# Three edits in the seams of a fused decoder kernel: when the second up pass's weights are loaded, where the first down product stands, and idle transposes at the start

## The chip, the cores and the metric

The kernel runs on one core of one Trainium2 chip. The metric is the device time of one execution in microseconds. Times of before are the median of three runs; a profile is one further execution, taken with the hardware profiler.

## The reference

The layer takes `x` (16 x 112 rows of 1024) and `ctx` (16 x 375 rows of 1024), all fp32, and does three steps, each followed by a residual sum and a layer norm:

```python
# 1. gated MLP with a sparse gate (I = 2752)
s = silu(x @ w_gate.T)                       # 1792 x 2752
_, idx = top_k(-abs(s), 1376)                # the smaller half of each row ...
s = s.at[rows, idx].set(0.0)                 # ... is set to zero
y = (s * (x @ w_up.T)) @ w_down.T            # called h below: s * up
x = layernorm(x + y)
# 2. cross attention: 32 heads of 32, 8 key and value heads, softmax over 375 keys
x = layernorm(x + attention(x, ctx) @ Wo)
# 3. an int4 weight, unpacked with scales and zeros, in bf16
x = layernorm(x + x.astype(bf16) @ dequantized.T)
```

## The kernel before

The 1792 rows are 14 tiles of 128 (`TT = 14`). Everything runs on one core, and the order of the instructions on each engine is the order in which the program writes them (`as_written` ties each instruction to the one before it on its engine). Nothing is reordered later, so an instruction that waits holds up all that stands behind it on its engine. That holds for SP too, whose queue issues most DMAs.

**Stages.** First the gate: for each tile six chunks of columns, each 8 logical matmuls over the contraction, 16 on the engine, since an fp32 matmul is run as two (line 190). The chunk's sigmoid is taken on ScalarE (L199), multiplied on VectorE (L200) and stored to `s_d` in DRAM by GpSimd's queue (L201). Then the up product, by a Strassen scheme on pairs of tiles: four passes over the columns (`UPASS = 4`), seven pairs of tiles in each, so 28 units; each unit is seven products (`up_unit`, L297) of four logical matmuls. Then keys and values (`kv_unit`, L367 and L375), amid which h is formed: GpSimd multiplies s by its mask (`next_turn`, L421), TensorE transposes the chunk (`turn`, L439), ScalarE copies it out of PSUM (L441, L445) and SP stores it to `hT_d` (L213). Then the down product (class `Down`, L725), again by Strassen, then the layer norm, the query projection, attention, and the quantized layer.

**The search beside it.** From the second tile on, ScalarE and VectorE search each row's median of |s| bit by bit (`count`, L468 and L471; `update`, L479 and L480), and `beside` interleaves this search with the TensorE stream. A product's evacuation from PSUM stands in the program one stream step behind the product (`settle(1)`), among the search's own instructions. There are six PSUM banks for products (`ps_g`) and two for transposes (`ps_t`).

**The swap.** When the gate's weights are no longer needed, `swap` gives their space to the up stage and issues on SP, in this order: `load_rest(0)` (tile xl of unit 0, L252 and L253), `load_weights(1)` (the four weight blocks of pass 1, L229). The first step of unit 0 then issues four loads of s (`load_s`, tile us, L276) and, in `side_loads(0)`, `load_first(1)` (tile xe of unit 1, L245 and L246) and `load_rest(1)`. Weights of pass p are combined by GpSimd in `sum_weights(p)` (L239); for pass 1 that is at unit 2, and pass 1 begins at unit 7. Pass 0's weights were loaded earlier, during the gate. Later passes' weights are asked for at the second unit of the pass before.

**The turn to the down product.** At the end of `gates_up_keys` a loop runs `next_turn` until every chunk of h has been asked for, with the stores that fall due (`issue(0)`). Then `down.first_blocks()` issues the loads of the first three blocks of h (L711, L712). A second loop finishes the turns that are still open, and a last `issue(0)` their stores. Then `first_passes` runs the 14 products of the first two Strassen terms, in the order of `self.order`, with three blocks ahead; at each step SP issues one more block and three loads of the other half's weights (`b12`, `b22`, L768). These weights lie in space that the up stage's tiles had. At the step `s == 9` VectorE combines them (L732, L741). Each product is 11 logical matmuls, 22 on the engine.

**The start.** `load_x(0)` (L162) issues the first tile of x, then nine DMAs issue the gate's weights, the first chunk in four pieces (L586); the matmuls begin when the first piece has landed. `ident`, the identity for transposes, is made by GpSimd ahead of that.

Of the kernel before, what the change touches and what calls it, by code (L numbers as in the profile page):

```python
# [10 lines left out]
F32 = mybir.dt.float32  # L11
# [11 lines left out]
P = 128  # L23
# [24 lines left out]
UPASS = 4  # L48
# [58 lines left out]
def gates_up_keys(  # L107
# [37 lines left out]
    def room(pool, tag, name, size, *shape, bufs=1):  # L145

        a = pool.tile([P, size], F32, tag=tag, name=name, bufs=bufs)
        n = 1
        for d in shape:
            n *= d  # L150
        a = a[:, :n]
        if len(shape) == 2:
            return a.rearrange("p (a b) -> p a b", b=shape[1])
        if len(shape) == 3:
            return a.rearrange("p (a b c) -> p a b c", b=shape[1], c=shape[2])
        return a
# [3 lines left out]
    def load_x(t):  # L160
        xts[t] = room(io, "e", f"xT_{t}", 4 * KH * P, KC, P, bufs=2)
        nc.sync.dma_start(xts[t], xT[t])  # L162
# [48 lines left out]
    def issue(behind=2):  # L211
        while stores and stores[0][0] >= len(stream) + behind:
            nc.sync.dma_start(*stores.popleft()[1:])  # L213
# [6 lines left out]
    def load_weights(p):  # L220

        if p % 2:
            u = room(upool[0], "w0", f"u0_{p}", 3 * KH * UW, 3, KH, UW)
            v = room(upool[0], "w1", f"u1_{p}", 4 * KH * UW, 4, KH, UW)
        else:
            u = room(lo, "lo0", f"u0_{p}", 5120, 3, KH, UW)
            v = room(lo, "lo1", f"u1_{p}", 5632, 4, KH, UW)
        for to, k, h in ((u[:, 0], 0, 0), (u[:, 2], 0, 1), (v[:, 0], 1, 0), (v[:, 1], 1, 1)):
            nc.sync.dma_start(to, wu[:, ts(k, KH), ds(h * FH + p * UW, UW)])  # L229
        w_up[p] = u, v  # L230

    def sum_weights(p):
        u, v = w_up[p]
        b11, t1, b12, b21, b22, t2, t4 = (
            z.rearrange("p k n -> p (k n)")
            for z in (u[:, 0], u[:, 1], u[:, 2], v[:, 0], v[:, 1], v[:, 2], v[:, 3])
        )
        for to, x, y in ((t1, b12, b11), (t2, b22, t1), (b12, b22, b12), (t4, b21, t2)):
            nc.gpsimd.tensor_tensor(to, x, y, ALU.subtract)  # L239

    def load_first(i):

        j = i % pairs
        a = first[i] = room(io, "e", f"xe_{i}", 4 * KH * P, 4, KH * P, bufs=2)
        nc.sync.dma_start(a[:, :2], xT[2 * j].rearrange("p (h k) n -> p h (k n)", h=2))  # L245
        nc.sync.dma_start(a[:, 2:], xs_d[j].rearrange("p h k n -> p h (k n)")[:, :2])  # L246

    def load_rest(i):

        j = i % pairs  # L250
        a = rest[i] = room(upool[0], "l", f"xl_{i}", 3 * KH * P, 3, KH * P, bufs=2)
        nc.sync.dma_start(a[:, :2], xs_d[j].rearrange("p h k n -> p h (k n)")[:, 2:])  # L252
        nc.sync.dma_start(a[:, 2], xT[2 * j + 1][:, KH:].rearrange("p k n -> p (k n)"))  # L253

    def side_loads(i):
        if i + 1 < n_up:
            load_first(i + 1)
            load_rest(i + 1)
        p, at = divmod(i, pairs)
        if at == 1 and 0 < p < UPASS - 1:  # L260
            load_weights(p + 1)
        if at == (4 if p else 2) and p < UPASS - 1:
            sum_weights(p + 1)
        if i == n_up - 4:
            load_keys()
# [13 lines left out]
    def up_unit(i, what):  # L279
# [10 lines left out]
        if what == "A11 B11":  # L290
            if i == 0:
                for _ in range(4):
                    load_s()
            side_loads(i)
# [49 lines left out]
    def load_keys():  # L344
        kv["k"] = upool[0].tile([P, KC, KVD], F32, tag="wk", name="wk_sb")
        nc.sync.dma_start(kv["k"], wk)
        load_ctx(0)
# [67 lines left out]
    def next_turn():  # L415

        if ready:
            turn(*ready.popleft())
        if asked:
            t, c, s, m = asked.popleft()  # L420
            nc.gpsimd.tensor_tensor(s, s, m, ALU.mult)  # L421
            ready.append((t, c, s))
        load_turn()
        if len(asked) < 2:
            load_turn()
# [122 lines left out]
    def swap():  # L548
        w_ctx.close()
        upool.append(w_ctx.enter_context(tc.tile_pool(name="u_w", bufs=1, side="right")))  # L550
        load_rest(0)
        load_weights(1)

    stream = deque()
    for t in range(TT):
        for c in range(len(GATE_CHUNKS)):
            stream.append((GATE_CHUNKS[c][1], lambda t=t, c=c: gate_chunk(t, c)))
    stream.append((0, swap))
    for i in range(n_up):
        for what in ("A11 B11", "S2 T2", "A12 B21", "S1 T1", "S4 B22", "S3 T3", "A22 T4"):  # L560
# [20 lines left out]
        return w  # L581

    load_x(0)
    for off, w in GATE_CHUNKS:
        for k in ([ts(i, 2) for i in range(KC // 2)] if off == 0 else [slice(0, KC)]):
            nc.sync.dma_start(wg_sb[:, k, ds(off, w)], wg[:, k, ds(off, w)])  # L586
# [53 lines left out]
    while to_turn:  # L640
        next_turn()
        issue(0)
    down.first_blocks()
    while asked or ready:
        next_turn()
    issue(0)
# [3 lines left out]
class Down:  # L650
# [99 lines left out]
    def bank(self, name):  # L750
        return self.ps.tile([P, 512], F32, tag="pg", name=name)

    def first_passes(self):
        nc, tc = self.nc, self.tc
        acc = self.left.enter_context(tc.tile_pool(name="d_acc", bufs=1, side="left"))
        with ExitStack() as ctx:
            self.a2 = ctx.enter_context(tc.tile_pool(name="d_a2", bufs=1, side="left"))
            w = ctx.enter_context(tc.tile_pool(name="d_w", bufs=1, side="right"))
            n = self.pairs
            b12, b22, t2 = (w.tile([P, HK, 512], F32, tag=k, name=k) for k in ("b12", "b22", "t2"))  # L760
            self.c11, self.u, self.v = (
                [acc.tile([P, 512], F32, tag=f"{k}{j}", name=f"{k}_{j}") for j in range(n)]
                for k in ("c11", "u", "v")
            )

            def load_chunk(to, i, k):
                r = P if k < FULL else REST
                nc.sync.dma_start(to[:r, k, :], self.wd[ds(i * FH + k * P, r), 512:])  # L768

            others = deque((to, i, k) for k in range(HK) for i, to in enumerate((b12, b22)))  # L770
            for s, (j, h) in enumerate(self.order):
                if s + 3 < len(self.order):
                    jj, hh = self.order[s + 3]
                    self.ahead.append(self.block(2 * jj, hh))
                for _ in range(min(3, len(others))):
                    load_chunk(*others.popleft())
                if s == 9:
                    self.combine(nc.vector, b12, b22, b12, ALU.subtract)
                    self.combine_parts(
                        "11", lambda k, t: t2[:, k : k + t.shape[1]],  # L780
                        lambda k, t: b12[:, k : k + t.shape[1]], lambda k, t: t, ALU.add,
                    )
                if s == len(self.order) - 3:
                    self.load_sums(0)
                a = self.ahead.popleft()
                p = self.bank(f"m{1 + h}_{j}")
                self.product(p, a, lambda k: self.chunk(("11", "21")[h], k))
                if h == 0:
                    nc.scalar.copy(self.u[j], p)
                else:  # L790
                    nc.vector.tensor_add(self.c11[j], self.u[j], p)
            self.combine_parts(
                "11", lambda k, t: t, lambda k, t: b22[:, k : k + t.shape[1]],
                lambda k, t: t2[:, k : k + t.shape[1]], ALU.subtract,
            )
            self.combine_parts(
                "21", lambda k, t: t, lambda k, t: t2[:, k : k + t.shape[1]],
                lambda k, t: t, ALU.subtract,
            )
            for j in range(n):  # L800
                if j + 1 < n:
                    self.load_sums(j + 1)
                else:
                    self.a2 = None
                    self.load_rest(0)
                s2, s3, s4 = self.live.pop(j)
                p, q, r = (self.bank(f"m{i}_{j}") for i in (6, 3, 7))
                self.product(p, s2, lambda k: t2[:, k, :])
                nc.vector.tensor_add(self.u[j], self.u[j], p)
                self.product(q, s4, lambda k: b22[:, k, :])  # L810
                nc.vector.tensor_add(self.v[j], self.u[j], q)
                self.product(r, s3, lambda k: b12[:, k, :])
                nc.vector.tensor_add(self.u[j], self.u[j], r)
# [659 lines left out]
```

## Time and profile before

| | |
|---|---|
| median of 3 runs | 2603.91 us (2603.18 to 2606.75) |
| the profiled execution | 2605.19 us |
| its span, first to last instruction | 2603.4 us |
| mean granted TensorE clock | 0.987 |
| PE (matmul) busy | 97% of the span |
| VectorE, ScalarE, GpSimd busy | 66%, 53%, 46% |
| DMA | 478.65 MB, mean 184 GB/s |

The stages lie in the span as follows: gate from 6 to 526 us, up from 526 to 991, keys and values from 991 to 1361, down from 1375 to about 1846, attention and the quantized layer from there on. In the rows of the profile PE is a matmul or a transpose, PEld a weight load, DVE is VectorE, ACT ScalarE, POOL GpSimd, and SPq an issue on SP's queue. A timeline row gives start, length, engine, line, operation, tiles, and in brackets the idle time of the engine before it and what ended it. A stretch row gives the stretch, its length, the busy time and number of instructions of PE, PEld, DVE, ACT and POOL, the granted TensorE clock, the share of the DMA engines and GB/s. Busy times of PE are modelled in part; starts are more exact than ends.

### The profile page before, as it was taken

Reading aid. Unit: us, or ns where it says so; the run is one execution under the profiler, and the core shown is the slowest. Engines: PE = TensorE matmul, PEld = TensorE weight load, DVE = VectorE, ACT = ScalarE, POOL = GpSimd, SP = SyncE. Lnnn points to the kernel's source line nnn. Section 1 sums busy time; section 2 is a strip of 40 time slices with the busy share of each in tenths; the row PEclk is TensorE's granted clock in tenths of the full one; section 3 lists DMA queues with packets and bytes.
Section 4 is the critical chain, followed back from the end, with each engine's and each line's share of the span. In section 5 each row is a group of like instructions: output and inputs, shape, how many; then the busy total and the mean of one; then the engine's idle time right before and its main releaser. Section 6 shows DMA issues by size and latency. Waiting matters only on the chain.

```text
span 2603.4 us, 34755 instructions
## 1 busy us (share of the span) xinstructions
PE 2520.8 (97%) x10490; PEld 1524.5 (59%) x10490; DVE 1721.1 (66%) x3634; ACT 1390.9 (53%) x2470; POOL 1205.0 (46%) x1143
## 2 busy tenths in 40 slices
PE   9999999999999999999989999999889999999996
PEld 4444444456666666777764444444556666666763
DVE  0378778868888897677740343247577777777773
ACT  0487787767767877888830000000355555555652
POOL 1113333256457544454250000024387888878883
PEclk9999999999999999999998999999999999999998
DMA  6322322277768768988657223157587777777763
GB/s 243 134 70 87 109 105 84 88 254 239 233 228 278 232 232 274 302 282 290 224 173 254 87 85 111 54 189 231 148 209 186 204 187 198 192 194 197 193 178 95
DMA packets 283609, 478.65 MB, mean 184 GB/s; under 512 B 37856, under 2 KB 208224, under 8 KB 279328
## 3 DMA queue, kind: packets, MB, share of 16 engines
q1 hardware_dynamic: 241184, 374.06, 46.9%
q0 software_dynamic: 27008, 75.76, 9.4%
q10 hardware_dynamic: 15232, 26.62, 3.4%
q8 instruction: 85, 1.39, 0.2%
q14 instruction: 100, 0.82, 0.1%
HBM read 272.12 MB, written 103.50 MB: 144 GB/s over the span
## 4 chain that ended last, share of the span: by engine, by line
PE 49%; DMA 7%; DVE 6%; POOL 3%; ACT 3%; issue 3%; SPq 1%; ACTq 0%; POOLq 0%; DVEq 0%
PE m L725 14%; PE pu L297 7%; PE bank L1105 6%; PE bank L946 5%; PE pk L375 4%; PE pk L367 4%; PE sc L1013 3%; PE po L1068 3%; DMA weights<-squares 2%; PE bank L1156 2%; ACT probs L1021 1%; DMA hT_d<-hT 1%; DMA hm<-m_d 1%; DVE jv L471 1%; SPq L1055 1%
## 5 line engine op out<-in xcount | busy, mean ns | idle before, releaser
L468 ACT ACTIVATE ja<-a,cand 128x1824 int8<-128x1824 f32 x434 | 787.9, 1815 | 197.1 <-DVE cand L480 189.2
L471 DVE TENSOR_SCALAR_CACHE_REDUCE jv<-a,cand 128x928 uint8<-128x928 f32 x434 | 509.7, 1174 | 43.7 <-ACT a L455 36.7
L190 PE MATMUL pg<-wg_sb,xT 128*128 128x456 f32 (+1 forms) x1344 | 520.0, 550 | 6.0 <-DMA wg_sb<-in_wg_dram 6.0
L190 PEld LDWEIGHTS pg<-wg_sb,xT 128*128 128x128 f32 x1344 | 256.6, 191 | 268.7 <-issue 265.6
L1021 ACT ACTIVATE probs<-sc,nmax 128x375 f32<-128x375 f32 x512 | 286.3, 572 | 229.6 <-DVE nmax L1019 213.2
L1030 POOL TENSOR_TENSOR probs<-probs,sums 128x1500 f32<-128x1500 f32 x128 | 344.1, 2689 | 134.5 <-DVE sums L1029 91.5
L1019 DVE TENSOR_REDUCE nmax<-sc 128x2 f32<-128x750 f32 x256 | 228.5, 932 | 129.4 <-PE sc L1013 129.4
L297 PE MATMUL pu<-u,xe 128*128 128x344 f32 x896 | 265.9, 455 | 6.6 <-DMA xe<-in_xT_dram 4.3
L725 PE MATMUL m<-wd,h 128*128 128x512 f32 (+1 forms) x616 | 267.7, 597 | 2.6 <-DMA h<-hT_d 2.6
L1041 DVE STREAM_TRANSPOSE squares<-probs 128x1536 f32<-128x1536 f32 x128 | 224.0, 1750 | 20.8 <-DMA weights<-squares 10.3
L297 PEld LDWEIGHTS pu<-u,xe 128*128 128x128 f32 x896 | 170.9, 191 | 97.7 <-DVE cand L480 5.0
L201 POOL DMA_DIRECT2D s_d<-s x84 | 45.9, 546 | 361.5 <-DVE s L200 296.5
L946 PE MATMUL bank<-x1T,wq_sb 128*128 128x224 f32 x1008 | 210.1, 362 | 0.0
L946 PEld LDWEIGHTS bank<-x1T,wq_sb 128*128 128x128 f32 x1008 | 188.0, 192 | 34.2 <-issue 31.3
L725 PEld LDWEIGHTS m<-wd,h 128*128 128x128 f32 (+1 forms) x616 | 117.8, 192 | 151.2 <-issue 150.2
L297 PE MATMUL pu<-u,xl 128*128 128x344 f32 x672 | 199.6, 453 | 1.8 <-DVE c L330 1.4
L1105 PE MATMUL bank<-wo_sb,aT 128*128 128x256 f32 x832 | 194.6, 388 | 0.0
L939 ACT COPY x1T<-pq 128x448 f32<-128x448 f32 x4 | 1.9, 535 | 349.1 <-DMA sc<-in_qs_dram 330.9
L1105 PEld LDWEIGHTS bank<-wo_sb,aT 128*128 128x128 f32 x832 | 155.2, 191 | 45.8 <-issue 23.3
L1055 POOL DMA_DIRECT2D weights<-squares x320 | 177.9, 562 | 6.9 <-PE po L1068 2.4
L375 PE MATMUL pk<-wv_sb,ctx 128*128 128x256 f32 (+1 forms) x768 | 173.3, 379 | 0.0
L421 POOL TENSOR_TENSOR hs<-hs,hm 128x512 f32<-128x512 f32 (+1 forms) x84 | 97.8, 1173 | 161.8 <-DMA hm<-m_d 143.8
(150 smaller groups left out, 3369.0 us busy)
## 6 DMA issues: line engine op xcount, KB each, us to landing
weights<-squares SPq DMA_DIRECT2D x704, 96.0 KB, 3.5
h<-hT_d SPq DMA_DIRECT2D x56, 640.0 KB, 4.6
weights<-squares POOLq DMA_DIRECT2D x320, 96.0 KB, 3.6
ctx<-in_ctxT_dram SPq DMA_DIRECT2D x16, 1500.0 KB, 8.3
a<-s_d SPq DMA_DIRECT2D x14, 1376.0 KB, 8.3
us<-s_d SPq DMA_DIRECT2D x112, 172.0 KB, 3.9
u_d<-c SPq DMA_DIRECT2D x84, 172.0 KB, 3.5
xe<-in_xT_dram SPq DMA_DIRECT2D x28, 512.0 KB, 5.3
```

The source lines that it names most:

```text
L190: nc.tensor.matmul(pg[:, :w], xts[t][:, kc, :], wg_sb[:, kc, ds(off, w)], start=(kc == 0), stop=(kc == KC - 1),)
L297: nc.tensor.matmul(m, a[i][:, b, ts(n, P)], k[:, n, :], start=(n == 0), stop=(n == KH - 1))
L375: nc.tensor.matmul(pk[:n, :KVD], c[:, kc, ds(at, n)], kv["v"][:, kc, :], start=(kc == 0), stop=(kc == KC - 1),)
L468: nc.scalar.activation(ja, a[:, NV:], AF.Sign, bias=cand, scale=-1.0, accum_out=st["sgn"])
L471: nc.vector.tensor_scalar(jv, a[:, :NV], cand, -(TOPK - 1 - NA / 2), ALU.is_lt, ALU.add, accum_out=st["nlt"])
L725: self.nc.tensor.matmul(bank, a[:r, k, :], b(k)[:r], start=(k == 0), stop=(k == HK - 1),)
L946: nc.tensor.matmul(pq[:, :GT], self.wq_sb[:, kc, ts(mc, P)], self.x1T[g][:, kc, :], start=(kc == 0), stop=(kc == KC - 1),)
L1019: nc.vector.tensor_reduce(nmax[h], sc[h][:, :, :SK], AX.X, ALU.max, negate=True)
L1021: nc.scalar.activation(pr[:, i, :SK], sc[i // 2][:, i % 2, :SK], AF.Exp, bias=nmax[i // 2][:, i % 2 : i % 2 + 1], accum_out=sums[:, i : i ...
L1030: nc.gpsimd.tensor_tensor(pr, pr, sums.unsqueeze(2).to_broadcast([P, 4, SK]), ALU.mult)
L1041: nc.vector.transpose(sq[:, :, n % 2].rearrange("p k (i f) -> p k i f", f=Q), probs[:, n % 3].rearrange("p i (k f) -> p k i f", f=Q),)
L1105: nc.tensor.matmul(pp[:, :256], aT[:, h, r, :], wo_sb[:, h * REP + r, ts(i, 256)], start=(h == 0 and r == 0), stop=(h == 1 and r == REP - 1),)
```

## The change

Three edits:

1. `load_weights(1)` is no longer called in `swap`. It is called in `side_loads(0)`, so behind the us loads and behind `load_first(1)` and `load_rest(1)` on SP.
2. The first of the 14 products of `first_passes` is moved into a method `first_product`, which is called behind `first_blocks()` and ahead of the loop that finishes the last turns. Its evacuation stays in `first_passes`.
3. Behind `load_x(0)`, 24 transposes of `ident` into a PSUM tile that nobody reads are written, ahead of all other work of TensorE.

```diff
@@ side_loads
-        if at == 1 and 0 < p < UPASS - 1:
+        if at == (1 if p else 0) and p < UPASS - 1:
             load_weights(p + 1)
@@ swap
         load_rest(0)
-        load_weights(1)
@@ gates_up_keys
     load_x(0)
+
+    idle = ps_t.tile([P, 512], F32, tag="pt", name="idle")
+    for _ in range(24):
+        nc.tensor.transpose(idle[:, :P], ident, ident)
     for off, w in GATE_CHUNKS:
...
     down.first_blocks()
+    down.first_product()
     while asked or ready:
         next_turn()
     issue(0)
@@ Down
+    def first_product(self):
+
+        self.first = self.bank("m1_0")
+        self.product(self.first, self.ahead.popleft(), lambda k: self.chunk("11", k))
...
-                a = self.ahead.popleft()
-                p = self.bank(f"m{1 + h}_{j}")
-                self.product(p, a, lambda k: self.chunk(("11", "21")[h], k))
+                if s == 0:
+                    p = self.first
+                else:
+                    a = self.ahead.popleft()
+                    p = self.bank(f"m{1 + h}_{j}")
+                    self.product(p, a, lambda k: self.chunk(("11", "21")[h], k))
                 if h == 0:
                     nc.scalar.copy(self.u[j], p)
```

## The prediction

> **What bounds the kernel now.** I read the page first, then the waits of TensorE, then the three places that the diff touches in the timeline, with granted clock and DMA by stretch.
>
> ```profile
> PE 2520.8 (97%) x10490; PEld 1524.5 (59%) x10490; DVE 1721.1 (66%) x3634; ACT 1390.9 (53%) x2470; POOL 1205.0 (46%) x1143
> ```
>
> PE works 97% of 2603.4 us, so an edit pays only where PE stands still or runs slowly. Its few idle stretches include all three places.
>
> The swap from gates to up (timeline of PE and SP, then stretches with PEclk):
>
> ```profile
> 535.10 7.11 PE L297 MATMUL pu<-u,xl 128*128 128x344 f32 x24
> 546.53 11.18 PE L297 MATMUL pu<-u,xe 128*128 128x344 f32 x32 [4.33 <-DMA xe<-in_xT_dram]
> ...
> 526.41 1.03 SPq L253 DMA_DIRECT2D xl<-in_xT_dram  x1
> 527.48 2.89 SPq L229 DMA_DIRECT2D u<-in_wu_dram  x4
> 530.63 6.71 SPq L276 DMA_DIRECT2D us<-s_d  x4
> 537.38 0.49 SPq L245 DMA_DIRECT2D xe<-in_xT_dram  x1
> ...
> 547.40:550.80 3.40, 3.40 (x7) 2.02 (x6) 2.92 (x10) 1.38 (x3) 2.60 (x3) 0.50 1.06 400
> 550.80:554.20 3.40, 3.40 (x13) 2.21 (x12) 1.00 (x2) 3.37 (x4) 0.00 (x0) 1.00 1.03 393
> ```
>
> Unit 0 ends at 546.53 - 4.33 = 542.20, and unit 1 waits for its operands (xe), queued behind four weight loads of pass 1. Then the clock is at 0.50 for one window: 7 matmuls where the next window has 13.
>
> What the search does there (timeline of ACT):
>
> ```profile
> 533.92 0.55 ACT L199 ACTIVATE s<-pg 128x456 f32<-128x456 f32 x1 [6.70 <-DMA s_d<-s]
> 567.05 0.45 ACT L315 COPY c<-pu 128x344 f32<-128x344 f32 x1 [5.11 <-issue]
> ```
>
> At 567.05 ACT takes unit 2's first product. It had been free since 561.94: it waited for PE, so PE is last there.
>
> The turn from h to the down products (PE, SP; then an earlier turn that waits for its PSUM bank):
>
> ```profile
> 1368.13 2.23 PE L439 MATMUL pt<-ident,hs 128*128 128x128 f32 x8 [0.21 <-POOL hs L421]
> 1371.34 0.90 PE L439 MATMUL pt<-ident,hs 128*128 128x128 f32 x3 [0.98 <-POOL hs L421]
> 1374.84 2.05 PE L725 MATMUL m<-wd,h 128*128 128x512 f32 x2 [2.60 <-DMA h<-hT_d]
> ...
> 1368.37 0.85 SPq L213 DMA_DIRECT2D hT_d<-hT  x2
> 1369.27 0.42 SPq L711 DMA_DIRECT2D h<-hT_d  x1
> 1373.49 2.91 SPq L213 DMA_DIRECT2D hT_d<-hT  x4
> ...
> 1042.35 0.52 PE L439 MATMUL pt<-ident,hs 128*128 128x128 f32 x3 [0.71 <-ACT hT L441]
> ```
>
> The four stores from 1373.49 belong to the last three turns (4 + 4 + 3 transposes), which now lie behind the product. The product waits for h, not for them: h is issued at 1369.27, right behind two stores of the turn before, and lands at 1374.71.
>
> The start (timeline of PEld; the DMA issues; stretches):
>
> ```profile
> 14.75 0.45 PEld L190 LDWEIGHTS pg<-wg_sb,xT 128*128 128x128 f32 x2 [0.33 <-DMA wg_sb<-in_wg_dram]
> wg_sb<-in_wg_dram SPq DMA_DIRECT2D x1, 1856.0 KB, 11.5
> ...
> 1366.60:1370.00 3.40, 2.77 (x11) 1.90 (x11) 0.00 (x0) 1.44 (x4) 2.59 (x3) 0.50 0.88 283
> 1376.80:1380.20 3.40, 3.40 (x6) 1.33 (x5) 0.00 (x0) 0.00 (x0) 0.00 (x0) 0.50 1.03 355
> ```
>
> Matmuls begin at 5.97 and start every 0.77 us until 11.51, then every 0.386: half clock, then full. Sixteen make a chunk. The second chunk's weights, issued at 3.20, land 11.5 us later, at 14.71, and its first weight load waits for them.
>
> **Step 1, weights of pass 1 later.** Nothing is added or removed; four loads of 688 KB move on SP behind the four us loads, xe and xl of unit 1. Ahead of xe's first half then lie xl (512 + 256 KB) and us (4 x 172 KB); with itself 1,968 KB. At the 322 GB/s of the stretch 526 to 542 that takes 6.3 us, at two thirds of that rate 9.4; from 526.04, and some 2 us for the landing (2.2 is the shortest of the s_d stores here), xe is there between 534 and 538. It is needed at 542.20, so the wait of 4.33 goes with 4 us to spare, and without an idle window the clock has no reason to fall: 3.40 us at half clock do 1.70 us of work, so 1.70 more. Together **-6.0**. Bounds: -4.3, if the half-clock window comes up anyway, to -6.9, as the half clock could last another half window.
>
> What is late next: the weights. They land last, no later than the last of the same bytes lands today (xl at 549.6). Their reader is sum_weights(1) on POOL, at 562.59 now and some 6 earlier then: 7 us of cover. Behind the four issues on SP stand the next us loads, u_d stores and unit 2's xe (545.42 now, landing 552.2). Unit 2 would start at 542.20 + 56 x 0.289 = 558.4, so 6 us of cover, and if it were gone each us would be paid in full. The search must keep up: ACT's waits for PE ahead of 561.94 (2.02 and 0.51) go, so it could be free at 559.4, while unit 2's first product is ready at 561.0. PE stays last, and the gain runs on. I take -6.0.
>
> **Step 2, first product ahead of the last three turns.** PE's instructions are the same, in another order; no DMA is added. The issue of h stays where it was, behind the stores of a turn that isn't moved, so the product still starts at 1374.84 and no gain is possible from an earlier start. What goes is the cover: 11 transposes that ran in the wait for h now run after the product, with PE busy on both sides (its longest idle stretches from 1374.84 to 1846 are under 0.5). At full clock they start every 0.107 us: 1.2. Back to back, the third turn needs the PSUM bank of the first (two buffers), which ACT has still to copy out: its copy takes 0.58 and starts 0.2 behind the transposes, the second turn covers 0.43 of it, so some 0.4 stays. Together **+1.6**; from 1.2 (no wait) to 2.9 (the longest wait of a turn for ACT in the trace, 1.74, in place of the 0.4).
>
> On SP the four stores now wait for the end of the product (about 1387), and behind them the fourth h block (1376.46 now) and 22 loads of b12 and b22 (from 1381.06), which want the landings of these stores: all some 13 us later. The fourth block is wanted after three products, at about 1407, and would land near 1396; the loads now end at 1413.3, the DVE combine that reads them starts at 1463.5. Both covers hold; I count nothing.
>
> **Step 3, idle transposes.** ident is ready at 1.30. The cold transposes at 1368.39 to 1368.82 start every 0.215: 24 end near 6.5, 0.6 behind the first matmul of now. If they don't raise the clock, 0.6 of half-clock work is lost until the rise at 11.51, so the second chunk starts 0.3 late. If they do, the first chunk ends 2.6 earlier and PE stands before the landing at 14.71: the gain is at most 15.01 - 14.94 = 0.1. The nearest row speaks against the rise: in 1366.60 to 1370.00 transposes alone kept PE busy 2.77 of 3.40 us and the clock stayed at 0.50, while a window full of matmuls (1376.80) ended at 1.00. That row is not quite full, so it leaves room. I take **+0.3**, bounds -0.6 (another phase of the windows) to +1.9 (below). [...]
>
> **The sum.** -6.0 + 1.6 + 0.3 = -4.1. The profiled execution took 2605.19 (span 2603.4 and 1.8 around it) and would take 2601.1. It is 1.3 above the median of the runs, 2603.91; the same difference from there gives **2599.8**. About 0.2%, 5.2 us, is what a measurement of this kernel can tell from no change: the forecast lies just inside it.
>
> **Rivals.**
> - *The idle transposes raise the clock, and it falls again.* The first chunk ends near 12.2, PE stands 2.5 us, the window 11.5 to 14.9 is nearly empty as 1363.20 to 1366.60 was (0.00 busy, then 0.50), and the second chunk runs half cold to 18.3: 1.7 lost, 0.1 won. Total -2.8: 2601.1. For it: PE is busy for a whole window; against: the row of transposes alone. Chance 0.15.
> - *Slower: the search becomes last at the swap.* ACT stood 6.70 us before 533.92, because its s tile waits for a store to s_d that took 6.2 us among SP's loads. The same bytes are in flight afterwards. If the store lands d later, ACT reaches unit 2 at 559.4 + d, and from d = 1.6 the gain shrinks; at d = 7.6 all of step 1 is gone and steps 2 and 3 stay: +1.9, 2605.8. [...] Chance 0.08.
> - *Half the swap's gain.* The wait goes, and the half-clock window turns up elsewhere: -2.4, 2601.5. Chance 0.12.
> - *The product does fill the turns' waits.* Were h in SBUF at 1368, the product would use the 0.98 and 2.60 us of idleness and begin in them: -3.6 in place of +1.6, total -9.3: 2594.6. SP's order speaks against it. Chance 0.05.
>
> **How the numbers follow.** My forecast has 0.60, and with the cold windows elsewhere in the kernel, which shift with everything, its own range is 2597 to 2602.5. The range of 2595.5 to 2605.0 takes in the first and third rival and leaves out most of the slower and the fastest. Faster by over 0.2% means below 2598.7: a third of the forecast's own chance, 0.20, the last rival and what a longer half clock brings, together 0.33. Slower by over 0.2% needs a stall that no row shows: 0.06. The rest, 0.61, lies within.
>
> **What would show it.** Right: no PE wait at unit 1 and PEclk 1.00 there; L229 on SP behind L245 and L252; unit 2 some 6 us earlier; L725 still waiting for h near 1369 to 1371, with 11 L439 transposes behind 22 matmuls; second chunk at 14.9 to 15.4. Wrong: a PE wait near 558 for xe or u; L725 starting before the stores of the turn before; a half-clock window at 15 to 18.

## The result, and the profile after

| | before | after |
|---|---|---|
| median of 22 runs each, us | 2604.25 (2598.11 to 2616.90) | 2600.17 (2594.01 to 2607.02) |
| ratio of the times | 1 | 0.9981, 95% interval 0.9972 to 0.9989 |
| span of the profiled execution, us | 2603.4 | 2596.7 |

The ratio is worth -4.9 us (-7.3 to -2.9), the medians differ by 4.1. The forecast was -4.1 and 2599.8, within 0.2% of before; the ratio measured lies 0.19% below 1, with an interval that reaches to both sides of 0.2%. That the medians differ by just the 4.1 that was forecast is chance: the interval is 4.4 us wide.

The page's line of busy times, after:

```profile
PE 2517.4 (97%) x10500; PEld 1526.5 (59%) x10514; DVE 1719.4 (66%) x3634; ACT 1390.3 (54%) x2470; POOL 1205.1 (46%) x1143
```

PE's busy share is the same 97%. Of the 6.7 us by which the span is shorter, 3.4 are busy time by this line and 3.3 idle time; the split is rough, as 14 matmul records are missing after (10500, where 10514 weights were loaded). No work was taken away: the idle transposes were added. To see where the time went, I cut both spans at four first starts on PE: the first up matmul, the first key product, the last key or value product, and the third down product.

| stretch, us | before | after | difference |
|---|---|---|---|
| start to the first up matmul (step 3 lies here) | 525.85 | 527.52 | +1.67 |
| to the first key product (step 1) | 465.68 | 460.07 | -5.61 |
| keys and values | 369.53 | 369.17 | -0.36 |
| last of these to the third down product (step 2) | 35.42 | 35.40 | -0.02 |
| the rest | 1206.9 | 1204.5 | -2.4 |

**The swap.** Timelines of PE, SP and ACT after, in the columns of the prediction's rows:

```profile
527.52 9.42 PE L297 MATMUL pu<-u,xe 128*128 128x344 f32 x32
...
543.72 9.42 PE L297 MATMUL pu<-u,xe 128*128 128x344 f32 x32
...
559.91 5.37 PE L297 MATMUL pu<-u,xe 128*128 128x344 f32 x18
```

```profile
529.18 1.90 SPq L276 DMA_DIRECT2D us<-s_d  x4
531.13 0.46 SPq L245 DMA_DIRECT2D xe<-in_xT_dram  x1
533.27 6.92 SPq L229 DMA_DIRECT2D u<-in_wu_dram  x4
545.24 0.38 SPq L245 DMA_DIRECT2D xe<-in_xT_dram  x1
```

```profile
533.17 0.55 ACT L199 ACTIVATE s<-pg 128x456 f32<-128x456 f32 x1 [4.28 <-DMA s_d<-s]
562.47 0.45 ACT L315 COPY c<-pu 128x344 f32<-128x344 f32 x1 [4.46 <-issue]
```

Units 0, 1 and 2 start at 527.52, 543.72 and 559.91, 16.2 us apart, and no bracket stands behind them: the wait of 4.33 is gone. L229 now stands behind L245 of unit 1. The two stretches of after around 543.72 (the last three numbers are granted clock, DMA share and GB/s):

```profile
541.30:544.70 3.40, 3.40 (x13) 2.21 (x13) 3.29 (x12) 3.37 (x6) 0.65 (x1) 1.00 1.04 388
544.70:548.10 3.40, 3.40 (x14) 2.21 (x13) 3.19 (x13) 3.37 (x5) 2.72 (x4) 1.00 1.07 382
```

These two stretches have 13 and 14 matmuls at a clock of 1.00, where before had 7 at 0.50. ACT still stands 4.46 us before it takes unit 2's first product, so PE is still last there.

**The turn from h to the down products**, PE and SP after:

```profile
1362.48 0.90 PE L439 MATMUL pt<-ident,hs 128*128 128x128 f32 x3 [4.91 <-POOL hs L421]
1369.52 11.58 PE L729 MATMUL m<-wd,h 128*128 128x512 f32 x22 [6.13 <-DMA h<-hT_d]
1380.94 1.04 PE L439 MATMUL pt<-ident,hs 128*128 128x128 f32 x8
1382.35 0.52 PE L439 MATMUL pt<-ident,hs 128*128 128x128 f32 x3 [0.37 <-ACT hT L441]
1382.71 17.77 PE L729 MATMUL m<-wd,h 128*128 128x512 f32 x41
```

```profile
1363.82 0.90 SPq L213 DMA_DIRECT2D hT_d<-hT  x2
1364.77 0.42 SPq L715 DMA_DIRECT2D h<-hT_d  x1
1382.23 1.93 SPq L213 DMA_DIRECT2D hT_d<-hT  x4
1384.22 0.43 SPq L715 DMA_DIRECT2D h<-hT_d  x1
1385.72 1.29 SPq L777 DMA_DIRECT2D b<-in_wd_dram  x3
```

The product is 22 matmuls that begin when h lands, as before, with a longer wait in front of them (6.13) since no transposes fill it. The 11 transposes then take 1382.71 - 1380.94 = 1.77 us with PE busy on both sides. The four stores, the fourth h block and the b loads follow on SP only at 1382 to 1386, and no PE wait comes of that.

**The start**, PE after, and its stretches (length; busy time and number for PE, PEld, DVE, ACT, POOL; clock; DMA):

```profile
1.36 4.40 PE L586 MATMUL idle<-ident 128*128 128x128 f32 x24 [1.36 <-POOL ident masks.py:199]
5.92 6.46 PE L190 MATMUL pg<-wg_sb,xT 128*128 128x464 f32 x16 [0.16 <-DMA wg_sb<-in_wg_dram]
14.95 6.57 PE L190 MATMUL pg<-wg_sb,xT 128*128 128x464 f32 x12 [2.57 <-DMA wg_sb<-in_wg_dram]
```

```profile
1.20:4.61 3.41, 3.25 (x15) 3.25 (x16) 0.23 (x1) 0.81 (x1) 0.10 (x1) 1.00 0.79 258
...
11.43:14.84 3.41, 0.95 (x3) 0.19 (x1) 0.64 (x1) 0.56 (x1) 0.75 (x1) 1.00 1.05 393
14.84:18.25 3.41, 3.30 (x5) 1.54 (x6) 0.00 (x0) 0.00 (x0) 0.00 (x0) 0.50 1.07 395
```

The transposes start every 0.213 us until 4.61 and every 0.107 from there: they brought full clock by themselves. (The 1.00 of the first row is no reading: ahead of the first change that the trace records the view shows 1.00, and the spacing is what tells the clock.) The first chunk is then done at 12.38, PE stands 2.57 us for the second chunk's weights, and behind a window with 0.95 us of work the clock is at 0.50 until 18.3. That is the first rival of the prediction, to its numbers, and the half-clock window at 15 to 18 that the prediction had named as a sign of being wrong.

### The profile page after: what moved, and what is told of

It is laid out like the page before. It is cut to its first block, busy times and chain, and to the rows that moved or that the text cites. A ratio compares the mean times of both kernels' runs of the same rounds, so it can differ in the third digit from the quotient of the medians.

```text
span 2596.7 us, 34788 instructions
## 1 busy us (share of the span) xinstructions
PE 2517.4 (97%) x10500; PEld 1526.5 (59%) x10514; DVE 1719.4 (66%) x3634; ACT 1390.3 (54%) x2470; POOL 1205.1 (46%) x1143
## 5 line engine op out<-in xcount | busy, mean ns | idle before, releaser
L1053 DVE STREAM_TRANSPOSE squares<-probs 128x1536 f32<-128x1536 f32 x128 | 224.0, 1750 | 20.3 <-DMA weights<-squares 10.4
```

The lines of the kernel that those rows point to most:

```text
L1053: nc.vector.transpose(sq[:, :, n % 2].rearrange("p k (i f) -> p k i f", f=Q), probs[:, n % 3].rearrange("p i (k f) -> p k i f", f=Q),)
```

## The experiments

Each run's ratio is against runs of the kernel before on the same chip, and the us beside it are that ratio times their median. Stretches are those of the table above.

### Each edit alone

**e1, edit 1 alone**: the hunks of `side_loads` and `swap`.

> Edit 1 alone: pass 1's weights behind unit 1's operands; the start and the first down product as before. Theory (the parts add up: -6.0 for the swap, +1.6 for the product's place, +0.3 to +1.7 for the idle transposes): 6 us faster than before, near 2598; no PE wait at unit 1, no half-clock window there, unit 0 begins at 525.9 and unit 2 near 558.4; the first L725 product still starts behind the last transposes and is over some 6 us earlier. Rival 'half the gain': the half clock comes up elsewhere, 4.3 faster. Rival 'the search takes it': PE waits for banks between 555 and 600, gain under 2.

Ratio 0.9978 (0.9967 to 0.9989), -5.7 us. Unit 0 starts at 525.79, the stretch to the first key product is 459.34. Units 1 and 2 start at 541.99 and 558.18, with no wait.

**e2, edit 2 alone**: `first_product()` behind `first_blocks()`.

> Edit 2 alone: the first down product ahead of the last three turns, all else as before. Theory: the product still starts where h lands (near 1374.8, PE idle some 6 us before it), the 11 transposes and a wait for a PSUM bank stand behind it; the second product starts 1.6 to 1.8 us later: 1.6 slower in total. Rival 'it fills the waits': 3 to 4 faster. Rival 'SP's later stores cost': over 5 slower, with a PE wait for an h block or VectorE late for its combine.

Ratio 1.0014 (1.0004 to 1.0024), +3.6 us (1.0 to 6.2): a loss. The turn looks as it does in after: a wait of 5.55 us for h, the product at 1374.54, the transposes at 1386.84, 0.37 us of wait for ACT, and the next product at 1388.61. 1388.61 - 1386.84 is 1.77 again. The interval of the loss holds that; the 1.8 us by which its middle lies higher are not accounted for by any row.

**e3, edit 3 alone**: the 24 idle transposes.

> Edit 3 alone: 24 idle transposes at the start, all else as before. Theory, revised from the trace of the changed kernel: the transposes do raise the clock (near 4.6 to 8), the first chunk of matmuls is over near 12, PE waits 1.5 to 2.6 us for the second chunk's weights (landing near 14.8), and where the window of that wait is nearly empty the clock halves for one window: unit 0 of the up stage starts 0 to 1.7 us later than 525.85, total 0.5 to 1.7 slower. Rival of the prediction: no rise, 0.3 slower. Rival 'it pays': 0.1 to 1 faster.

Ratio 1.0002 (0.9990 to 1.0013), +0.5 us (-2.6 to +3.4). Its profiled execution went the other way from after. PE, and its stretches:

```profile
14.79 6.50 PE L190 MATMUL pg<-wg_sb,xT 128*128 128x464 f32 x16 [2.08 <-DMA wg_sb<-in_wg_dram]
```

```profile
9.52:12.93 3.41, 3.18 (x9) 1.24 (x7) 0.00 (x0) 0.19 (x1) 0.00 (x0) 1.00 1.05 394
12.93:16.34 3.41, 1.55 (x4) 0.87 (x5) 0.64 (x1) 0.37 (x1) 0.75 (x1) 1.00 1.05 391
```

The clock rose at 6.07, still ahead of the first matmul (6.31), and stayed: the wait of 2.08 us fell astride two windows, with 3.18 and 1.55 us of work in them. Unit 0 started at 525.73, 0.12 ahead of before; in the nine traces without idle transposes at the start it starts at 525.79 to 526.39. So the same code cost 1.67 in one execution and nothing in another; the first rise stands at 4.61 in the one and at 6.07 in the other.

**e10, edits 1 and 2 without the idle transposes.**

> The changed kernel without edit 3 (edits 1 and 2 alone). Theory by the stages (-6.4 up to the first key product, +1.4 at the turns): 4 to 5.5 faster than before, unit 0 of the up stage at 525.9 instead of 527.5; the same as the changed kernel within 2 us, since the idle transposes cost it from -0.2 to 1.6. Rival 'the idle transposes pay': slower than the changed kernel, under 3.5 faster than before.

Ratio 0.9981 (0.9973 to 0.9990), -4.9 us: the same as the whole change. Edit 3 does nothing that these runs can measure. The totals of e1, e2 and e3 add up to -1.6 us, each with some 3 us of interval on either side: that does not contradict -4.9, and it does not resolve the single terms either. For those the stretches of the traces have to serve.

### Is it the clock that the start is about?

**e4, edit 3 and a bridge** of 24 more idle transposes between the first chunk and the second:

```diff
-    for _ in range(2 * len(GATE_CHUNKS) + 1):
+    for i in range(2 * len(GATE_CHUNKS) + 1):
         emit()
+        if i == 0:
+            idle = ps_t.tile([P, 512], F32, tag="pt", name="idle_1")
+            for _ in range(24):
+                nc.tensor.transpose(idle[:, :P], ident, ident)
```

> Edit 3 and 24 more idle transposes behind the first chunk's matmuls, all else as before. Theory (the clock falls because PE stands still while the second chunk's weights land): 24 transposes at full clock take 2.6 us and fill that wait, the clock stays up, the second chunk starts at 14.9 to 15.0 at full clock and unit 0 of the up stage starts at 525.7 to 525.9: as fast as before within 0.3, some 1.5 faster than with edit 3 alone when that one falls. Rival 'the bridge costs its length': 2 slower than edit 3 alone.

PE, and the stretch that holds the bridge:

```profile
12.46 2.78 PE L596 MATMUL idle<-ident 128*128 128x128 f32 x24
15.18 6.11 PE L190 MATMUL pg<-wg_sb,xT 128*128 128x464 f32 x15
```

```profile
12.03:15.44 3.41, 3.41 (x27) 2.94 (x26) 0.64 (x1) 0.56 (x1) 0.75 (x1) 1.00 1.06 393
```

The bridge held the clock: 1.00 from 5.2 on, with no fall at 15. Yet unit 0 starts at 526.12, 0.27 behind before, and the ratio is 1.0013 (0.9998 to 1.0028), +3.4 us (-0.5 to +7.3). The second chunk starts at 15.18, since its weights land at 15.14 in this execution; they land at 14.71 in before, 14.74 in e3 and 14.90 in after, and the chunk starts behind them each time (15.01, 14.79, 14.95). With the clock kept, the 1.67 us that after lost were not lost, but nothing was won over before: the DMA is last there. The rival of 2 us does not show in the trace (unit 0 is 0.39 behind e3), though the totals alone could not exclude it.

### How far can the weights of pass 1 move?

**e7, the weights one unit later** than in edit 1 (alone, on before): `if at == 1 and p < UPASS - 1`, so behind unit 2's operands.

> Edit 1 with the weights of pass 1 one unit later still: behind unit 2's operands (issued near 545 to 550 instead of 533). Theory (the weights have cover: they are read by GpSimd at unit 2, near 557 to 562, and by TensorE at unit 7): they land near 557 to 562, GpSimd's combine waits at most some us, TensorE doesn't; as fast as edit 1 alone within 1 us, 5 to 6 faster than before. Rival 'the cover is gone': GpSimd's products with s queue behind the combine, PSUM banks are freed late, PE waits for VectorE near 575 to 590; 2 or more slower than edit 1 alone.

Ratio 0.9987 (0.9976 to 0.9997), -3.4 us (-6.3 to -0.8) against e1's -5.7 (-8.6 to -2.9): the intervals overlap, so the trace has to tell. PE waits twice, and the longest waits ahead of these lead back to one row load (timelines of PE and of SP, then the waits: who, for whom, us in total, times, longest):

```profile
583.67 2.58 PE L297 MATMUL pu<-u,xe 128*128 128x344 f32 x8 [1.64 <-DVE c L324]
587.56 7.21 PE L297 MATMUL pu<-u,xl 128*128 128x344 f32 x24 [1.31 <-DVE u L328]
```

```profile
544.80 6.33 SPq L229 DMA_DIRECT2D u<-in_wu_dram  x4
554.47 0.38 SPq L452 DMA_DIRECT2D a<-s_d  x1
```

```profile
DVE jv L471 <- ACT a L455: 7.9, 1, 7.9
ACT a L455 <- DMA a<-s_d: 3.4, 1, 3.4
```

The two waits are 2.95 together, where e1 has 0.41 of the second and none of the first; the stretch to the first key product is 462.36, 3.0 over e1's 459.34. The weights themselves came in time. What was late is the search's next row tile `a`, whose load stands behind them on SP and is issued at 554.47, in e1 at 551.03. ACT waited 3.4 us for it, in e1 not at all; VectorE waited 7.9 for ACT, in e1 4.3; and the evacuations of pu (L324, L328) stand among the search's instructions.

### What is the turn's cost, and can it be a gain?

**e8, two products ahead of the last three turns** (on before): `first_product` loops over `self.order[:2]`. It doubles the time by which SP's stores, blocks and b loads are held back, and leaves the turns' cover as in e2.

> Edit 2 doubled, nothing else: the first two down products ahead of the last three turns. Edit 2 alone came out 3.6 us slower (1.0 to 6.2), where its trace shows 1.8 at the turns. Theory (the cost is the transposes' lost cover, paid once): the same 1.8 us at the turns, now behind the second product; total 1 to 4 slower than before, as with one product. Rival 'the cost is SP's queue behind the late stores': SP stands some 9 us longer, the fourth h block lands near 1403 for a product that wants it at 1408, and total is 5 or more slower.

```profile
1377.48 21.81 PE L726 MATMUL m<-wd,h 128*128 128x512 f32 x44 [6.96 <-DMA h<-hT_d]
1399.13 1.04 PE L439 MATMUL pt<-ident,hs 128*128 128x128 f32 x8
```

Ratio 1.0003 (0.9993 to 1.0012), +0.8 us (-1.8 to +3.1): the expected loss of 1 to 4 can't be told from none in the total. The next product starts at 1400.90, so the turns cost 1.77 once more. SP's stores are issued at 1400.43 and the next block at 1402.41, counted from the first product's start 24 and 23 us later than in before (1373.49 and 1376.46, with the product at 1374.84), and still no PE wait follows. So SP's queue is not what costs time in edit 2, as far as the trace shows.

**e5, the loads of h ahead of the turn before** (with edit 1), so that h is not issued behind that turn's stores:

```diff
+    down.first_blocks()
     while to_turn:
         next_turn()
         issue(0)
-    down.first_blocks()
+    down.first_product()
     while asked or ready:
```

> Edit 1, and the first three h blocks are asked for on SP ahead of the loop that asks for the last chunks of h; the first product stands where the change puts it, ahead of the last three turns. In the run of edit 1 alone the h loads were issued at 1362.4 and the first product started at 1366.7, the second at 1379.2. Theory (what held the product was SP's order, not the transposes): h is issued near 1354 and lands near 1360, the product starts right behind the turn before (near 1361), 5 to 6 earlier, the turns behind it cost 1.6: the second product starts 3.5 to 5 us earlier than with edit 1 alone; total 9 to 11 faster than before, near 2593. Rival 'the hs and hm loads behind six h loads come late': the last turns move, no more than 6 faster, near 2597.

**e6, as e5, with the product ahead of that turn as well**: `if len(to_turn) == 1: down.first_product()` inside the loop.

> As the run with the blocks asked for early, and the first product stands ahead of the last four turns instead of three, so ahead of the turn for which TensorE waited 4.9 us. Theory: the product starts when h lands (near 1360), and no turn stands ahead of it; 0.5 to 1.5 better than with three turns behind it, total 10 to 12 faster than before. Rival 'the longer delay of the turns' stores reaches an h block or the combine': a PE wait in the first products, slower than with three.

e5: 0.9953 (0.9940 to 0.9967), -12.2 us (-15.6 to -8.6). e6: 0.9960 (0.9948 to 0.9973), -10.4 (-13.5 to -7.0). With e9 below, these are the fastest kernels measured. The profiled execution of e5 is the slowest of its five (2598.29): its keys and values took 373.4 us, in e1 369.2, so that its span is no shorter than e1's, and only its stretch at the turn can be compared. PE in e1, which has edit 1 but the old turn, and in e5:

```profile
1354.58 0.60 PE L439 MATMUL pt<-ident,hs 128*128 128x128 f32 x4
1360.11 0.90 PE L439 MATMUL pt<-ident,hs 128*128 128x128 f32 x3 [4.94 <-POOL hs L421]
1361.22 2.23 PE L439 MATMUL pt<-ident,hs 128*128 128x128 f32 x8 [0.21 <-POOL hs L421]
1364.21 0.90 PE L439 MATMUL pt<-ident,hs 128*128 128x128 f32 x3 [0.76 <-POOL hs L421]
1366.67 33.74 PE L724 MATMUL m<-wd,h 128*128 128x512 f32 x71 [1.56 <-DMA h<-hT_d]
```

```profile
1358.72 0.60 PE L439 MATMUL pt<-ident,hs 128*128 128x128 f32 x4
1365.18 0.90 PE L439 MATMUL pt<-ident,hs 128*128 128x128 f32 x3 [5.86 <-POOL hs L421]
1366.02 11.39 PE L725 MATMUL m<-wd,h 128*128 128x512 f32 x22
1377.25 1.04 PE L439 MATMUL pt<-ident,hs 128*128 128x128 f32 x8
1379.02 6.17 PE L725 MATMUL m<-wd,h 128*128 128x512 f32 x14
```

From the last key or value product (1354.36 and 1358.51) the first down product comes after 12.31 us in e1 and after 7.52 in e5: 4.8 won. In e5 it carries the turns, 1.77, but less of it runs at half clock (in e5's record until 1369.5, in e1's until 1372.8; 11.23 us to its end against 12.54): 1.3 more won. 4.8 + 1.3 - 1.8 = 4.3, and the stretch to the third product is 34.30 in e1 and 29.97 in e5. Against the expectation, h was not there near 1360: counted from the last key or value product it was issued 7.9 us earlier than in e1 but landed only 4.8 earlier (at 1365.89, 7.2 us after its issue; 4.2 in e1), and the turn ahead waited 5.86 us for its chunk, in e1 4.94. So e6, in which that turn no longer stands ahead, wins nothing on e5: 30.05. What is left of the distance between e1's -5.7 and e5's -12.2 no row accounts for; their intervals end at -8.6 on both sides, so it may be spread.

**e9, e6 with 56 idle transposes** in front of the product, where PE stands 6.33 us for h.

> As the run with the first product ahead of four turns, and 56 idle transposes in front of that product (6.0 us at full clock), in the wait for h that lasted 6.33 us there and after which the product's first matmuls ran at half clock (the product took 11.4 instead of 9.4). Theory (transposes count as work for the clock, as the start of the changed kernel showed): no half-clock window near 1362, the product takes 9.4 to 9.6 us; up to 2 better than without the filling, 10 to 14 faster than before. Rival (transposes don't count, or only delay): the clock falls all the same, the product takes 11 us or more, 0 to 1 slower than without the filling.

PE's timeline and the stretch of that wait, first both for e6 and then both for e9:

```profile
1365.11 11.53 PE L726 MATMUL m<-wd,h 128*128 128x512 f32 x22 [6.33 <-DMA h<-hT_d]
```

```profile
1358.70:1365.10 6.40, 0.08 (x1) 0.02 (x1) 0.00 (x0) 1.23 (x3) 2.27 (x3) 0.76 1.01 319
```

```profile
1356.07 6.28 PE L644 MATMUL idle<-ident 128*128 128x128 f32 x56
1362.81 9.68 PE L729 MATMUL m<-wd,h 128*128 128x512 f32 x22 [0.46 <-DMA h<-hT_d]
```

```profile
1355.90:1362.80 6.90, 6.45 (x60) 6.23 (x58) 0.00 (x0) 1.23 (x3) 1.84 (x3) 1.00 0.97 322
```

The clock stays at 1.00, the product takes 9.68 us instead of 11.53, and the stretch to the third product is 28.45 against 30.05. In the total, 0.9963 (0.9951 to 0.9975) or -9.6 us (-12.8 to -6.5), the 1.6 us can't be seen beside e6's -10.4.

## Why the prediction was right

**Step 1 held: -6.0 forecast.** The stretch to the first key product is 459.2 to 460.1 us in the six traces that have edit 1 as the change has it (after, e1, e5, e6, e9, e10) and 463.7 to 466.1 in the five without (before, e2, e3, e4, e8). Their means differ by 5.7, before and e1 by 6.3. From unit 0 to unit 2 it is 38.64 us before and 32.39 after, 6.25 less: the whole wait and the whole half-clock window. Before's wait of 4.33 is the longest of the five traces without the edit (3.12 to 4.33), hence the lower mean. So the rival of half the gain fell. xe landed at 536.49 in e1, whose unit 0 starts as in before, within the 534 to 538 of the working. The slower rival fell too: with the weights later on SP, ACT's wait for the store, which GpSimd's queue issues, went from 6.70 to 4.28 us (4.82 in e1), so the store came sooner, not later. One cover had been named wrongly. I had taken the weights' own reader as next to be late; e7 shows that the next is the search's row load behind them on SP.

**Step 2 held: +1.6 forecast, 1.77 in each of five traces** (after, e2, e5, e8, e10), of which 0.37 is the wait for the PSUM bank (0.4 forecast) and 1.40 the transposes (1.2 forecast). The table's -0.02 for this stretch hides it, for two reasons that vary from execution to execution. Before's own profiled execution waited 2.60 us for h, where e1, e3, e4 and e7, with the same code there, waited 1.56 to 1.84. And its first product ran at half clock for 5.4 us (until 1380.23), where after's did so for 3.8 (until 1373.35), which makes 0.8 us. Over all traces the stretch is 34.4 on average without the edit (before, e1, e3, e4, e7) and 35.9 with it (after, e2, e10; 37.2 in e8, with two products ahead). The product did not start earlier: 6.45 to 7.04 us after the turn ahead of it with the edit (7.86 in e8), 6.56 to 7.82 without. SP's order did speak against the rival by which the product fills the turns' waits. e5 changes that order, and there it does: 4.3 us, though h then took longer to land, 7.2 us from its issue against 4.2 in e1; no run shows why.

**Step 3 came out within its bounds by a mechanism I had rejected.** The term was +0.3, from the reading that transposes don't raise the clock. No run shows that term: unit 0 started 1.67 us later than before in after and 0.12 earlier in e3. Nor does the reading hold for the fp32 transposes here: the window 1.20 to 4.61 of after, with 3.25 us of transposes, ended at full clock, and e4 and e9 kept 1.00 with transposes. The failing step is the choice of row: in 1366.60 to 1370.00 PE was busy 2.77 of 3.40 us with transposes and the clock stayed at 0.50, and I took that for a trait of transposes, while the prediction itself noted that the window was not full. The first rival (chance 0.15) is what after's profile shows: 1.7 lost and 0.1 won forecast, +1.67 measured at unit 0. e3 shows that it isn't always so (-0.12), and e10 against the change that it averages out below what the runs can tell. So in these two traces the term is +1.67 and -0.12, and that +0.3 lies between them, for another reason than the one given, is luck. Where the windows lie differs: the first rise came at 4.61 in after, 6.07 in e3 and 5.22 in e4. Within after, the later changes lie whole multiples of 3.41 us behind the first (the next at 14.85, three windows on), and within before likewise (547.40 is 157 windows behind the rise at 11.51).

**The sum.** By the stretches: -5.7 to -6.3 + 1.8 + (-0.1 to 1.7) is -4.6 to -2.2, and the measured -4.9 (-7.3 to -2.9) overlaps with it. The profiled pair differs by more, 6.7. The 2.4 us on top lie in the attention and the quantized layer, which no edit touches. From the first score product to the start of PE's last instruction the twelve traces take 740.0 (e4) to 746.9 (e9), before 743.4, after 741.0, without regard to the edits: the executions' own spread.

## What to carry to other kernels

Moving a step into a wait pays only if what the wait is for comes no later and the step was not already filling that wait: count what had covered it, and find the issue that sets the landing (here SP's order, which e5 changed) before reordering the engine that waits. On an in-order queue, whoever stands behind the moved loads can be the next to be late, even when it belongs to another part of the kernel (e7: the search's row load, for which ACT waited 3.4 us). Filler that kept the clock up won nothing over before where a DMA ended last (e4: unit 0 0.27 us behind before), and 1.6 us of a stretch where the work behind the wait ran at half clock without it (28.45 in e9, 30.05 in e6).

## What the runs showed of the hardware

- fp32 transposes alone raised the TensorE clock and held it. In after, fifteen at half clock, 0.213 us apart from 1.36 on, with 3.25 us of work in the window, stood before full clock at 4.61; in before, the 2.77 us of transposes in the stretch from 1366.60 were followed by another stretch at 0.50. In e9, 56 of them held 1.00 through the wait, and the product behind them took 9.68 us in place of e6's 11.53.
- Two waits for the second chunk's weights ended differently. After's was 2.57 us long and left 0.95 us of work in the window of 3.41 us that it fell into, and the clock was 0.50 from 14.85 to 18.26; e3's was 2.08 us long and fell astride two windows, with 3.18 and 1.55 us of work in them, and the clock stayed at 1.00. The first rise stands at 4.61 in after and at 6.07 in e3.
